# Fetching embedding rows from ScalarE's queue as well, in a gather-bound recommendation kernel on one Trainium2 core

## The chip, the cores and the metric

The kernel runs on one core of one Trainium2 chip. The metric is the device time of one execution in microseconds. The kernel before takes 32,128.78 us, the median of three runs between 32,128.46 and 32,131.62. A core has five engines, each with an instruction stream of its own: TensorE (PE, with its weight loads as PEld), VectorE (DVE), ScalarE (ACT), GpSimd (POOL) and SyncE (SP), which here only issues transfers. They meet through semaphores. A suffix q (SPq, ACTq) marks what an engine's sequencer does itself, such as issuing a transfer.

## The reference

The model is an attention network over a user's history of 200 items. With B = 16384 users, L = 200 history positions, D = 64 features per item, and 36 hidden units in the attention unit:

```python
def dice(x, alpha, axis):
    mean = jnp.mean(x, axis=axis, keepdims=True)
    var = jnp.var(x, axis=axis, keepdims=True)
    p = jax.nn.sigmoid((x - mean) * jax.lax.rsqrt(var + EPS))
    return x * (p + alpha * (1.0 - p))
u, it, c, h = u_emb[user], i_emb[item], c_emb[cate], i_emb[hist]   # h: 200 x 16384 x 64
itb = jnp.broadcast_to(it[None], h.shape)
feat = jnp.concatenate([h, itb, h - itb, h * itb], axis=-1)
a = dice(feat @ au_W1 + au_b1, au_alpha, axis=1)     # mean and variance over the 16384 users
w = a @ au_W2 + au_b2
cur = jnp.sum(w * jax.lax.stop_gradient(h), axis=0)  # sum over the 200 positions
z = jnp.concatenate([u, it, c, cur], axis=-1)
z = dice(z @ W1 + b1, alpha1, axis=0)
z = dice(z @ W2 + b2, alpha2, axis=0)
return z @ W3 + b3
```

The item table has 100,000 rows of 64 floats, 256 bytes each. Fetching 200 x 16384 = 3.28 million such rows from memory, in random order, is the bulk of the data movement (840 MB of the 882 MB that the profile counts).

## The kernel before

For each history position l the 16384 users are 128 tiles of 128 users. Sixteen tiles make one step, so that each l has ND = 8 steps; steps are numbered k = 8 l + c through the whole kernel, c from 0 to 7.

*Fetching.* A step's rows go into one of five buffers `rows`, [128 users, 16 tiles, 64 features]. GpSimd fetches a tile with one indirect gather of 128 rows (`gather`, line 117), its indices in `idx`, which SP loads once per l. In the steps named in `SIDES` (c = 3 and c = 7) the sixteenth tile comes another way, "by address": SP loads the item numbers of these two tiles as integers (`load_addresses`, line 135), DVE multiplies them by the row's 256 bytes (line 138), SP reads 16 of them at a time into its registers (line 258), and issues one transfer of 256 bytes per row (line 265) into a small tile `side`. ACT then copies `side` into the place in `rows` (line 301). So an l has 126 gathers by GpSimd and 256 single-row transfers by SP.

*Computing.* A step's rows are turned by DVE (`transpose`, line 146) into `hT`, [128, 1024], with features on the partitions. TensorE forms the hidden layer in the PSUM tile `px` from three products (line 151): `blk_h` with `hT`, `blk_i` with the turned item rows `itT`, and, a moment later, `blk_m` with `hm`. ACT copies `hT` to the PSUM tile `ph` (line 304); DVE multiplies that with `itT` to give `hm` (line 307). ACT adds the bias and writes `xs` (`hidden`, line 290), DVE takes statistics of `xs` (line 295). After the eighth step of an l, DVE and ACT make mean and variance into a scale and a shift (`moments`). Ten steps after its fetch (LAG) a step is weighed: ACT takes the sigmoid of `xs` with that scale and shift into the PSUM tile `pg` (line 278), then applies an affine with per-partition numbers, p (1 - alpha) w2 + alpha w2 (line 279); DVE multiplies by `xs` to give `y` (line 282); TensorE sums over the hidden units with the 0/1 matrix `blk_w` into `wb`; and DVE adds the bias, multiplies by `hT` and accumulates into `curT` (lines 286, 287).

*Order.* The order on each engine is the one in which `step` and `steps` write it down (`manual_schedule`); the framework adds semaphore waits where data or buffers require them, and each engine runs its own stream strictly in order. In step k that order is: fetch k; gate and weights of k - 10; hidden and statistics of k - 2; turn of k - 1; weighing of k - 10; product of k - 1; and after the last step of an l, its moments. SP's rows are asked for in front of each step (`ask`), 32 of a tile's 128 rows per step. For each DMA of SP the framework rotates over eight semaphores, so a row's transfer waits for the one eight before it.

*Loop.* 45 positions l form the body of a hardware loop that runs four times (line 406); the remaining 20 follow, and then the head: user and category gathers, two dense layers with their statistics, and the result.

Of the kernel before, what the change touches and what calls it, by code (L numbers as in the profile page):

```python
# [9 lines left out]
I32 = mybir.dt.int32  # L10
AF = mybir.ActivationFunctionType
ALU = mybir.AluOpType
PSUM = bass.MemoryType.PSUM

P = 128
D = 64
EPS = 1e-8
CH = 512
S = 32
CD = 2 * CH  # L20
LPB = 45
ROWS = 5
LAG = 10
XR = 9
IDX = 3
SIDES = (3, 7)
LOAD = 16
ROW = 4 * D
U8 = mybir.dt.uint8

# [2 lines left out]
def din_kernel(  # L33
# [24 lines left out]
    nc = tc.nc  # L58
    L, B = r_hist.shape
    NT = B // P  # L60
    TD = 2 * CD // P
    ND = NT // TD
    V = i_emb.shape[0]
# [2 lines left out]
    ZA = P // 2  # L66
    ZB = Z1 - ZA
    NS = len(SIDES)
    NC = NT - NS
    BODY = L - L % LPB if L > LPB else 0  # L70
    STATS = nc.vector.BN_STATS_DIM
# [5 lines left out]
    def make(name, *shape, dt=F32):  # L77
        return const.tile(list(shape), dt, name=name)
# [4 lines left out]
    def quarter(e, g, n=S):  # L83
        return slice((2 * e + g) * S, (2 * e + g) * S + n)
# [11 lines left out]
    ph = psum.tile([P, CD], F32, name="ph")  # L96
    pg = psum.tile([P, CD], F32, name="pg")
    wb = psum.tile([P, CD], F32, name="wb")

    rows = [make(f"rows{i}", P, TD, D) for i in range(ROWS)]  # L100
# [4 lines left out]
    hm = make("hm", P, CD)  # L105
# [2 lines left out]
    idx = [make(f"idx{i}", P, NC, dt=I32) for i in range(IDX)]  # L108
    ids = [make(f"ids{i}", P, NT, dt=I32) for i in range(3)]
    side = [make(f"side{i}", P, D) for i in range(3)]  # L110
    addr = [make(f"addr{i}", 1, NS * P, dt=I32) for i in range(3)]
    stats = [make(f"st{i}", P, 2 * ND, STATS) for i in range(3)]
    rstds = [make(f"rs{i}", P, 1) for i in range(3)]
    shifts = [make(f"sh{i}", P, 1) for i in range(3)]
# [28 lines left out]
    def transpose(dst, of):  # L143
        for i in range(2):
            for e in range(2):
                nc.vector.transpose(by_tile(dst[ts(e, D)], i), of[ts(i, D), :, ts(e, S)])  # L146

    def layer(dst, pairs, first=True, last=True):
        for i in range(2):
            for j, (lhsT, rhs) in enumerate(pairs):  # L150
                nc.tensor.matmul(  # L151
                    dst[:, ts(i, CH)], lhsT, rhs[:, ts(i, CH)],
                    start=(first and j == 0), stop=(last and j == len(pairs) - 1),
                    skip_group_check=not (first and last),
                )
# [9 lines left out]
    blk_h = make("blk_h", P, P)  # L165
    blk_i = make("blk_i", P, P)
    blk_m = make("blk_m", P, P)
    blk_w = make("blk_w", P, P)
    au_w = make("au_w", P, 4, A)
    au_bias = make("au_bias", P, 1)  # L170
    au_al = make("au_al", P, 1)
# [4 lines left out]

    def attention_weights():
        nc.vector.memset(eps, EPS)
        for t in (blk_h, blk_i, blk_m, blk_w, au_bias, au_al, au_w2):
            nc.vector.memset(t, 0.0)  # L180
        nc.sync.dma_start(au_bias2, au_b2.partition_broadcast(P))
        for e in range(2):
            w = au_W1.rearrange("(g d) a -> d g a", d=D)[e * S : (e + 1) * S]
            for g in range(2):
                r = quarter(e, g)
                nc.sync.dma_start(au_w[r], w)
                for q, (a0, n) in enumerate(halves):
                    c, a = quarter(q, g, n), slice(a0, a0 + n)
                    nc.vector.tensor_add(blk_h[r, c], au_w[r, 0, a], au_w[r, 2, a])
                    nc.vector.tensor_sub(blk_i[r, c], au_w[r, 1, a], au_w[r, 2, a])  # L190
                    nc.vector.tensor_copy(blk_m[r, c], au_w[r, 3, a])
                    nc.vector.memset(blk_w[r, quarter(q, g)], 1.0)
        for g in range(2):
            for q, (a0, n) in enumerate(halves):
                r, a = quarter(q, g, n), slice(a0, a0 + n)
                nc.sync.dma_start(au_bias[r], col(au_b1)[a])
                nc.sync.dma_start(au_al[r], col(au_alpha)[a])
                nc.sync.dma_start(au_w2[r], au_W2[a])
        nc.vector.tensor_scalar(au_1al, au_al, -1.0, 1.0, ALU.mult, ALU.add)
        nc.vector.tensor_mul(au_1al, au_1al, au_w2)  # L200
        nc.vector.tensor_mul(au_al, au_al, au_w2)


    w1a = make("w1a", P, 4, P)
# [10 lines left out]
    al1a, al1b, al12 = make("al1a", P, 1), make("al1b", P, 1), make("al12", P, 1)  # L215
    same_a = make("same_a", P, P)
    same_b = make("same_b", P, P)
    lanes = make("lanes", P, P, dt=I32)
    lane = make("lane", P, P, dt=I32)

    def head_weights():
        for t in (w1a, w1b, w2a, w2b, w3, bias2, al2):
# [28 lines left out]

    flat = i_emb.rearrange("v d -> (v d)").bitcast(U8)

    def rows_by_address(m, l, part, n):
        s, dst = m % NS, side[m % 3].bitcast(U8)
        for b in range(0, n, LOAD):
            p0 = part * n + b
            _, at = nc.values_load_multi_w_load_instructions(  # L258
                addr[l % 3][:, s * P + p0 : s * P + p0 + LOAD],
                engines=(mybir.EngineType.SP,), min_val=0, max_val=ROW * (V - 1),  # L260
                skip_runtime_bounds_check_because="the DMA checks the address against the table",
            )
            for j, a in enumerate(at):
                p = p0 + j
                nc.sync.dma_start(dst[p : p + 1], flat[ds(a, ROW)].rearrange("(o d) -> o d", o=1))  # L265

    def has_side(k):
        return k % ND in SIDES
# [7 lines left out]
    def gate(k):  # L276
        i = k // ND % 3
        nc.scalar.activation(pg, xs[k % XR], AF.Sigmoid, bias=shifts[i], scale=rstds[i])  # L278
        nc.scalar.activation(pg, pg, AF.Identity, bias=au_al, scale=au_1al)  # L279

    def weights(k):
        nc.vector.tensor_mul(y, pg, xs[k % XR])  # L282
        layer(wb, [(blk_w, y)])

    def weigh(k):
        nc.vector.scalar_tensor_tensor(wb, wb, au_bias2, hT[k % LAG], ALU.add, ALU.mult)  # L286
# [5 lines left out]
    def measure(k):  # L292
        l, c = divmod(k, ND)
        for i in range(2):
            nc.vector.bn_stats(stats[l % 3][:, 2 * c + i, :], xs[k % XR][:, ts(i, CH)])  # L295

    def turn(k):
        if has_side(k):
            l, c = divmod(k, ND)
            m = l * NS + SIDES.index(c)  # L300
            nc.scalar.copy(rows[k % ROWS][:, TD - 1], side[m % 3])
        transpose(hT[k % LAG], rows[k % ROWS])
        layer(px, [(blk_h, hT[k % LAG]), (blk_i, itT[k % ND])], last=False)
        nc.scalar.copy(ph, hT[k % LAG])  # L304

    def product(k):
        nc.vector.tensor_mul(hm, ph, itT[k % ND])  # L307
# [22 lines left out]
    def step(k, last=None):  # L330

        def has(j):
            return last is None or j <= last

        if has(k):
            fetch(k)
        if has(k - LAG):
            gate(k - LAG)
            weights(k - LAG)
        if has(k - 2):  # L340
            hidden(k - 2)
            measure(k - 2)
        if has(k - 1):
            turn(k - 1)
        if has(k - LAG):
            weigh(k - LAG)
        if has(k - 1):
            product(k - 1)
        if has(k - 2) and (k - 2) % ND == ND - 1:
            moments((k - 2) // ND)  # L350

    PER = ND // NS

    def ask(k, end):
        m, part = divmod(k + 1, PER)
        if m < end * NS:
            rows_by_address(m, m // NS, part, P // PER)

    def steps(l0, n, end):
        for k in range(n * ND):
            l, c = divmod(k, ND)
            if c == 0 and l + 1 < end:
                load_hist_ids((l + 1) % IDX, l0 + l + 1)
            if c == 2 and l + 1 < end:
                load_addresses((l + 1) % 3, l0 + l + 1)
            if c == 4 and l + 1 < end:
                scale_addresses((l + 1) % 3)
            ask(k, end)  # L370
            step(k)

    with tc.manual_schedule():
        load_ids(ids[0], r_item)
        load_hist_ids(0, 0)
        load_addresses(0, 0)
        load_ids(ids[1], r_cate)
        load_ids(ids[2], r_user)
        nc.gpsimd.iota(lanes, pattern=[[1, P]], base=P, channel_multiplier=-1)
        attention_weights()  # L380
        for t in (*hT, *xs, *side, hm):
            nc.vector.memset(t, 0.0)  # L382
        for t in curT:
            nc.vector.memset(t, 0.0)
        for i in range(3):
            nc.vector.memset(rstds[i], 0.0)
            nc.vector.memset(shifts[i], 0.0)  # L387
        nc.vector.bn_stats(stats[-1 % 3][:, 0, :], hm[:, :CH])
        for c in range(1, 2 * ND):
            nc.vector.tensor_copy(stats[-1 % 3][:, c, :], stats[-1 % 3][:, 0, :])  # L390
        scale_addresses(0)
        layer(px, [(blk_m, hm)])

        for c in range(ND + 1):
            if c < ND:
                for n in range(TD):
                    j = column(c, n)
                    gather(rows[c % ROWS], ids[0][:, j : j + 1], n, i_emb)
            if c:
                transpose(itT[c - 1], rows[(c - 1) % ROWS])  # L400
        nc.vector.memset(rows[-1 % ROWS], 0.0)
        ask(-1, L)
        head_weights()

    if BODY:
        with tc.For_i(0, BODY, LPB) as l0:  # L406
            with tc.manual_schedule():
                steps(l0, LPB, LPB + 1)

    K = (L - BODY) * ND  # L410
    za = [hT[(K - LAG + c) % LAG] for c in range(ND)]
# [140 lines left out]
```

## Time and profile before

| | us |
|---|---|
| median of three runs | 32,128.78 |
| the profiled execution's own time | 32,101.94 |
| its span, first to last instruction | 32,100.2 |
| busy: PE (with PEld beside it) | 15,661.4 (6,253.8) |
| busy: DVE | 14,921.9 |
| busy: ACT | 7,823.3 |
| busy: POOL | 24,139.4 |
| gathers of history rows: count, mean | 25,200, 0.944 |
| row transfers by SP: count, median to issue one | 51,200, 0.225 |

A row of the groups of instructions reads: line, engine, operation, output and input tiles, shape, count, then busy time and mean in ns, and the idle time of that engine just before these instructions with what ended most of it. "issue" is time in which the engine waited for nothing that the profile shows. A row of the view of one line gives the shortest, median and longest duration in ns. A row of windows gives the stretch in us, its length, the busy time and count of the engine, the granted TensorE clock, the DMA engines' busy share and GB/s. A row of the timeline gives the start in us, the length, the engine, and the idle time before it; several equal instructions in succession stand in one row, with their count. A row of waits gives who waited for whom, the sum in us, how often, and the longest.

### The profile page before, as it was taken

How to read it: one execution, taken by the hardware profiler on the slowest of the kernel's cores; microseconds unless marked ns; L12 is line 12 of the kernel's file. 1: busy time of each engine (PE TensorE's matmuls, PEld its weight loads, DVE VectorE, ACT ScalarE, POOL GpSimd, SP SyncE). 2: the span in 40 equal slices, each digit the busy share in tenths (PEclk: the TensorE clock that was granted, in tenths of full speed). 3: DMA queues.
4: the chain of work that ended last, by engine and by line, in shares of the span. 5: the costliest groups of instructions: out<-in, count | busy, mean ns of one | idle time of the engine just before them, and what ended most of it. 6: DMA issues, size and time to landing. Idle time of an engine off the chain costs nothing. (4 is left out here: it accounts for less than half of the span.)

```text
span 32100.2 us, 224464 instructions
## 1 busy us (share of the span) xinstructions
PE 15661.4 (49%) x26020; PEld 6253.8 (19%) x26020; DVE 14921.9 (46%) x18956; ACT 7823.3 (24%) x7481; POOL 24139.4 (75%) x25589
## 2 busy tenths in 40 slices
PE   4444444444444444444445444454444444445445
PEld 1111121111111111111112111121111211112111
DVE  4444444444444444444444444444444444444443
ACT  2222222222222222222222222222222222222222
POOL 7777777777777777777777777777777777777776
PEclk7777767776777777777777777777777777777777
DMA  1111111111111111111111111111111111111111
GB/s 28 28 28 28 28 28 28 28 27 28 28 28 28 28 28 28 28 27 28 28 28 28 28 28 28 28 28 28 28 28 28 28 28 28 28 28 28 28 28 22
DMA packets 958596, 881.57 MB, mean 27 GB/s; under 512 B 547488, under 2 KB 547688, under 8 KB 957032
## 3 DMA queue, kind: packets, MB, share of 16 engines
q0 software_dynamic: 818688, 839.97, 11.8%
q1 hardware_dynamic: 138056, 27.05, 0.4%
q14 instruction: 1352, 11.08, 0.1%
q8 instruction: 212, 3.47, 0.0%
q10 hardware_dynamic: 288, 0.00, 0.0%
HBM read 865.03 MB, written 0.13 MB: 27 GB/s over the span
## 5 line engine op out<-in xcount | busy, mean ns | idle before, releaser
L117 POOL DMA_INDIRECT rows<-in_L_rec_i_emb,idx x25200 | 23776.6, 944 | 7706.1 <-issue 7132.8
L151 PE MATMUL px<-hT,blk_h 128*128 128x512 f32 x6404 | 5661.5, 983 | 15033.9 <-DVE hT L146 15033.9
L146 DVE STREAM_TRANSPOSE hT<-rows 64x512 f32<-64x512 f32 x6404 | 4519.1, 706 | 12085.3 <-DMA rows<-in_L_rec_i_emb,idx 11421.6
L304 ACT COPY ph<-hT 128x1024 f32<-128x1024 f32 x1601 | 1627.1, 1016 | 18738.7 <-DVE hT L146 18738.7
L151 PEld LDWEIGHTS px<-hT,blk_h 128*128 128x128 f32 x6404 | 1816.6, 314 | 18047.2 <-issue 17233.6
L151 PE MATMUL px<-itT,blk_i 128*128 128x512 f32 x6404 | 4735.4, 832 | 0.0
L151 PE MATMUL wb<-y,blk_w 128*128 128x512 f32 x6440 | 3413.4, 657 | 1245.9 <-DVE y L282 1230.2
L295 DVE BATCH_NORM_STATS2 st<-xs 128x6 f32<-128x512 f32 x3204 | 2058.3, 684 | 3704.4 <-ACT xs L290 3704.4
L151 PE MATMUL px<-hm,blk_m 128*128 128x512 f32 x6408 | 3036.9, 596 | 38.1 <-DVE hm L382 36.4
L290 ACT ACTIVATE xs<-px,au_bias 128x1024 f32<-128x1024 f32 x1602 | 1781.6, 1112 | 4164.1 <-PE px L151 4164.1
L151 PEld LDWEIGHTS px<-itT,blk_i 128*128 128x128 f32 x6404 | 1862.1, 291 | 2859.9 <-issue 2859.9
L282 DVE TENSOR_TENSOR y<-pg,xs 128x1024 f32<-128x1024 f32 x1610 | 1954.9, 1214 | 736.6 <-ACT pg L279 736.4
L286 DVE SCALAR_TENSOR_TENSOR wb<-wb,au_bias,hT 128x1024 f32<-128x1024 f32 x1610 | 2081.1, 1293 | 82.2 <-PE wb L151 30.0
L287 DVE TENSOR_TENSOR curT<-wb,curT 128x1024 f32<-128x1024 f32 x1610 | 1971.2, 1224 | 54.8
L278 ACT ACTIVATE pg<-xs,sh,rs 128x1024 f32<-128x1024 f32 x1610 | 1937.3, 1203 | 79.9 <-DVE sh L387 42.7
L307 DVE TENSOR_TENSOR hm<-ph,itT 128x1024 f32<-128x1024 f32 x1601 | 1942.5, 1213 | 0.0
L279 ACT ACTIVATE pg<-pg,au_al,au_1al 128x1024 f32<-128x1024 f32 x1610 | 1895.1, 1177 | 54.1
L151 PEld LDWEIGHTS wb<-y,blk_w 128*128 128x128 f32 x6440 | 1307.8, 207 | 2976.1 <-issue 1538.0
L151 PEld LDWEIGHTS px<-hm,blk_m 128*128 128x128 f32 x6408 | 1195.9, 191 | 1686.8 <-issue 1236.5
L278 ACT ACT_TABLE_LOAD x206 | 264.3, 1283 | 77.5 <-PEq L406 57.4
L160 ACT ACT_TABLE_LOAD x203 | 260.4, 1283 | 7.5 <-PE pg L461 4.0
L160 ACT ACTIVATE std<-var,eps 128x1 f32<-128x1 f32 x201 | 59.2, 294 | 710.6 <-DVE var L327 710.6
(147 smaller groups left out, 1531.7 us busy)
## 6 DMA issues: line engine op xcount, KB each, us to landing
side<-in_L_rec_i_emb SPq DMA_DIRECT2D x51200, 0.2 KB
rows<-in_L_rec_i_emb,idx POOLq DMA_INDIRECT x25200, 2.4
idx<-in_r_hist SPq DMA_DIRECT2D x200, 63.0 KB
addr<-in_r_hist SPq DMA_DIRECT2D x200, 1.0 KB
rows<-in_L_rec_i_emb,ids POOLq DMA_INDIRECT x128, 2.4
rows<-in_L_rec_c_emb,ids POOLq DMA_INDIRECT x128, 2.3
rows<-in_L_rec_u_emb,ids POOLq DMA_INDIRECT x128, 2.4
w1a<-in_L_rec_W SPq DMA_DIRECT2D x4, 32.0 KB
```

The costliest lines, as they stand in the source:

```text
L117: nc.gpsimd.indirect_dma_start(out=dst[:, n, :], out_offset=None, in_=table, in_offset=bass.IndirectOffsetOnAxis(ap=ids, axis=0),)
L146: nc.vector.transpose(by_tile(dst[ts(e, D)], i), of[ts(i, D), :, ts(e, S)])
L151: nc.tensor.matmul(dst[:, ts(i, CH)], lhsT, rhs[:, ts(i, CH)], start=(first and j == 0), stop=(last and j == len(pairs) - 1), skip_group_c ...
L278: nc.scalar.activation(pg, xs[k % XR], AF.Sigmoid, bias=shifts[i], scale=rstds[i])
L279: nc.scalar.activation(pg, pg, AF.Identity, bias=au_al, scale=au_1al)
L282: nc.vector.tensor_mul(y, pg, xs[k % XR])
L286: nc.vector.scalar_tensor_tensor(wb, wb, au_bias2, hT[k % LAG], ALU.add, ALU.mult)
L287: nc.vector.tensor_add(curT[k % ND], wb, curT[k % ND])
L290: nc.scalar.activation(xs[k % XR], px, AF.Identity, bias=au_bias)
L295: nc.vector.bn_stats(stats[l % 3][:, 2 * c + i, :], xs[k % XR][:, ts(i, CH)])
L304: nc.scalar.copy(ph, hT[k % LAG])
L307: nc.vector.tensor_mul(hm, ph, itT[k % ND])
```

## The change

Two more tiles of each l are fetched by address, and ACT issues these. `SIDES` becomes (1, 3, 5, 7): SP takes the sixteenth tile of steps 1 and 5, ACT that of steps 3 and 7. GpSimd's gathers fall from 126 to 124 per l. In each step ACT issues four groups of eight rows (`GROUP`), two after the sigmoid and two after `hidden`; each group begins with a load of eight addresses into ACT's registers. The transfers increment a semaphore of the destination tile (`landed`), three tiles (`aside`) taking turns, and carry no waits of their own; before the copy of a tile ACT waits until all 128 rows have counted in, and clears the semaphore. The body of the loop ends with that wait for the tile still under way. SP's requests start two steps earlier (`AHEAD`), because its tiles are now used in steps 1 and 5. The addresses of all four tiles lie in one tile `addrs`, loaded and scaled in one instruction each as before.

ACT loses two instructions per step. The affine after the sigmoid is folded into TensorE's sum: `wb` becomes `blk_p` times p x plus `blk_x` times x, with the two per-partition numbers multiplied into the 0/1 matrix beforehand. The copy of `hT` to `ph` becomes a product of `hT` with a unit matrix, placed in front of the products into `px`. Both are fp32 products of [128 x 128] with two halves of 512 columns. The integer tiles `lanes` and `lane` of the head move into buffers that are free at that time.

```diff
-SIDES = (3, 7)
+BY_SP = (1, 5)
+BY_ACT = (3, 7)
+SIDES = (1, 3, 5, 7)
 LOAD = 16
+GROUP = 8
...
+    aside = [make(f"aside{i}", P, D) for i in range(3)]
+    landed = [tc.alloc_semaphore(f"landed{i}") for i in range(3)]
+    addrs = make("addrs", 2 * S + 1, NS * P, dt=I32)
+    addr = [addrs[i * S : i * S + 1] for i in range(3)]
...
+        nc.vector.tensor_scalar_mul(blk_x, blk_p, au_al)
+        nc.vector.tensor_scalar_mul(blk_p, blk_p, au_1al)
+        nc.vector.tensor_copy(unit, lanes)
+        nc.vector.tensor_single_scalar(unit, unit, float(P), ALU.is_equal)
...
+    def addresses(l, s, p0, n, engine):
+        _, at = nc.values_load_multi_w_load_instructions(
+            addr[l % 3][:, s * P + p0 : s * P + p0 + n],
+            engines=(engine,), min_val=0, max_val=ROW * (V - 1),
...
+        return [flat[ds(a, ROW)].rearrange("(o d) -> o d", o=1) for a in at]
+
+    def rows_by_sync(m, part, n):
+        l, j = divmod(m, NB)
+        s, dst = SIDES.index(BY_SP[j]), side[m % 3].bitcast(U8)
+        for p0 in range(part * n, part * n + n, LOAD):
+            for j, row in enumerate(addresses(l, s, p0, LOAD, mybir.EngineType.SP)):
+                nc.sync.dma_start(dst[p0 + j : p0 + j + 1], row)
+
+    keys = {}
+
+    def rows_by_scalar(m, part):
+        l, j = divmod(m, NA)
+        s, dst = SIDES.index(BY_ACT[j]), aside[m % 3].bitcast(U8)
+        key = keys.setdefault(m, f"rows{next(serial)}")
+        for j, row in enumerate(addresses(l, s, part * GROUP, GROUP, mybir.EngineType.Activation)):
+            p = part * GROUP + j
+            dma = nc.scalar.dma_start(dst[p : p + 1], row).then_inc(landed[m % 3], 16)
+            tc.no_tile_sem_insts.add(dma.ins.name)
+            tc.add_to_no_dep_group(key, dma.ins)
+
+    def await_rows_by_scalar(m):
+        if m in keys:
+            fence = nc.scalar.wait_ge(landed[m % 3], 16 * P)
+            tc.declare_fence(fence.ins, group=keys.pop(m))
+            nc.scalar.sem_clear(landed[m % 3])
...
     def gate(k):
         i = k // ND % 3
         nc.scalar.activation(pg, xs[k % XR], AF.Sigmoid, bias=shifts[i], scale=rstds[i])
-        nc.scalar.activation(pg, pg, AF.Identity, bias=au_al, scale=au_1al)
 
     def weights(k):
         nc.vector.tensor_mul(y, pg, xs[k % XR])
-        layer(wb, [(blk_w, y)])
+        layer(wb, [(blk_x, xs[k % XR]), (blk_p, y)])
...
-            m = l * NS + SIDES.index(c)
-            nc.scalar.copy(rows[k % ROWS][:, TD - 1], side[m % 3])
+            if c in BY_ACT:
+                m = l * NA + BY_ACT.index(c)
+                await_rows_by_scalar(m)
+                of = aside[m % 3]
+            else:
+                of = side[(l * NB + BY_SP.index(c)) % 3]
+            nc.scalar.copy(rows[k % ROWS][:, TD - 1], of)
         transpose(hT[k % LAG], rows[k % ROWS])
+        layer(ph, [(unit, hT[k % LAG])])
         layer(px, [(blk_h, hT[k % LAG]), (blk_i, itT[k % ND])], last=False)
-        nc.scalar.copy(ph, hT[k % LAG])
...
             gate(k - LAG)
             weights(k - LAG)
+        if has(k):
+            scalar_rows(k, 0)
         if has(k - 2):
             hidden(k - 2)
             measure(k - 2)
+        if has(k):
+            scalar_rows(k, 1)
         if has(k - 1):
             turn(k - 1)
...
-    PER = ND // NS
+    AHEAD = ND // NB - 1 - BY_SP[0]
 
     def ask(k, end):
-        m, part = divmod(k + 1, PER)
-        if m < end * NS:
-            rows_by_address(m, m // NS, part, P // PER)
+        m, part = divmod(k + 1 + AHEAD, ND // NB)
+        if m < end * NB:
+            rows_by_sync(m, part, P * NB // ND)
+
+    def scalar_rows(k, slot):
+        m, part = divmod(k, ND // NA)
+        n = P * NA // ND // GROUP
+        for i in range(n)[slot::2]:
+            rows_by_scalar(m, part * n + i)
...
-        ask(-1, L)
+        for k in range(-1 - AHEAD, 0):
+            ask(k, L)
...
                 steps(l0, LPB, LPB + 1)
+                await_rows_by_scalar(LPB * NA - 1)
```

## The prediction

> **What bounds the kernel now.** I read the page's rows first, then GpSimd's timeline, then the instructions of the two lines that fetch rows by address, then the waits. The page:
>
> ```profile
> span 32100.2 us, 224464 instructions
> ...
> POOL 7777777777777777777777777777777777777776
> ...
> L117 POOL DMA_INDIRECT rows<-in_L_rec_i_emb,idx x25200 | 23776.6, 944 | 7706.1 <-issue 7132.8
> ```
>
> POOL shows 75% busy, evenly, and its idle time is put down to "issue", its own dispatching. So the busy share understates it: every gather has 0.944 us of work and 0.30 us of issue. Two windows of 50 us and the end of one loop turn show the pace:
>
> ```profile
> 10037.00:10087.00 50.00, 37.80 (x41) 0.69 0.13 28
> 10100.00:10150.00 50.00, 37.81 (x41) 0.69 0.12 26
> ```
>
> ```profile
> 7238.83 0.94 POOL L117 DMA_INDIRECT rows<-in_L_rec_i_emb,idx  x1 [0.30 <-issue]
> 7240.08 0.94 POOL L117 DMA_INDIRECT rows<-in_L_rec_i_emb,idx  x1 [0.30 <-issue]
> 7249.02 0.94 POOL L117 DMA_INDIRECT rows<-in_L_rec_i_emb,idx  x1 [8.00 <-issue]
> ```
>
> Start to start a gather takes 1.249 us, as 7238.83 to 7240.08. The gathers number 25,584 (25,200 for history, 384 for the other tables): 25,584 x 1.249 = 31,954 us of a span of 32,100. Only four gaps between them exceed 1.4 us (8.9, 7.2, 7.2, 4.0 us): the three turns of the loop and its exit. The rest is the 2.9 us ahead of the first gather and some 135 us of head after the last. Gathers set the end; nothing that the others do inside a step shows. The waits agree: consumers wait for rows, on DVE and then on ACT.
>
> ```profile
> DVE hT L146 <- DMA rows<-in_L_rec_i_emb,idx: 11421.6, 1498, 9.3
> ACT ph L304 <- DVE hT L146: 18738.7, 1601, 13.5
> ACT xs L290 <- PE px L151: 4164.1, 1397, 3.8
> ```
>
> Each l has 8 steps and 126 gathers, so a step is now 126 / 8 x 1.249 = 19.67 us.
>
> **Fewer gathers.** Two gathers fewer for each of 200 l: 400 x 1.249 = 499.6 us saved, if the pace stays and nobody else becomes the bound. The new step is 124 / 8 x 1.249 = 19.36 us. Does more row traffic slow a gather? In the first of the two windows SP issued 121 row transfers, in the second none: both hold 41 gathers, and the spacings are 1.2491 and 1.2486 us. A second stream at the same price would cost 24,800 x 0.0005 = 12 us; I take 0 to 12, value 3.
>
> **ACT's new work.** Per step it issues 32 rows in four groups of 8, each led by a load of 8 addresses into registers (helper `addresses`). SP does the same now, in groups of 16:
>
> ```profile
> L265 SPq MOVE side<-in_L_rec_i_emb x51200: 29/29/38, 48.4 to 31504.5; - x200
> L265 SPq DMA_DIRECT2D side<-in_L_rec_i_emb x51200: 224/225/362, 48.5 to 31504.5; - x200
> ...
> L258 SPq TENSOR_LOAD <-addr x3200: 1130/1229/1483, 47.1 to 31498.1; - x189
> ...
> 10006.81 25.05 SPq L265 DMA_DIRECT2D side<-in_L_rec_i_emb  x64
> ```
>
> From one row's issue to the next is 0.32 us (move 0.029, DMA 0.225, dispatch), and a load of 16 addresses stretches that once by 1.30: 16 x 0.32 + 1.30 = 6.42, 0.40 a row, as 25.05 / 64 says. No row shows a load of 8. Above, it costs the 1.30 of 16. Below, the Trainium skill's DMA: Bandwidth & Descriptors, "Latency and other measured facts", gives a floor of about 0.6 us for such a load. ACT's step is 32 x 0.32 = 10.2 us plus 4 x 0.6 to 1.3: 12.6 to 15.4 us. I take 15.4, as the load's row is measured and its split per address is not.
>
> ACT's own arithmetic beside it: the sigmoid 1.20, `hidden` 1.11, side copies 4 x 0.23 / 8 = 0.12, two table loads per l 2 x 1.28 / 8 = 0.32, the square root 0.04: 2.8 us. The affine (1.18) and the copy to `ph` (1.02) go:
>
> ```profile
> L304 ACT COPY ph<-hT 128x1024 f32<-128x1024 f32 x1601 | 1627.1, 1016 | 18738.7 <-DVE hT L146 18738.7
> ...
> L279 ACT ACTIVATE pg<-pg,au_al,au_1al 128x1024 f32<-128x1024 f32 x1610 | 1895.1, 1177 | 54.1
> ```
>
> Is arithmetic added to issuing, or under it? Line 301's semaphore instructions start at 10072.7, when `hidden` has just started at 10072.69 and runs to 10073.80: ACT's sequencer goes on under a running ACTIVATE. So the sum is 15.4 us plus what an ACTIVATE waits before it starts; not overlapped at all it is 18.2. Both are under 19.36. What queues behind the rows: `hidden` of step k-2 stands after 16 of them (7.7 us), the side copy and the next sigmoid after the other 16; `measure` and the next turns on DVE wait for these. A turn can be late by about three steps, some 58 us, before POOL waits, because `rows` has five buffers. Only throughput counts. The `landed` wait stands about one step after its last row was issued, against some 2.4 us to landing for a gather: zero cost. At a turn of the loop ACT now ends at 7226.9, 13 us before POOL's last gather at 7240.1, with the copy to `ph`; that goes, and the groups in its place end about as late: zero. If ACT's slack were gone, each us over 19.36 costs 1600 us.
>
> **The shared descriptor generator.** A rule that speaks against this: the skill's Perfetto Trace Analysis, "DMA Instruction — HWDGE (DVE, Sync)", says that such a DMA locks one generator, shared by the two issuing engines, for exclusive use. SP issues 256 rows per l too. If all 0.225 us are lock, then while both issue a row takes 0.45, not 0.32. SP needs 256 x 0.45 + 16 x 1.30 = 136 us of 154.9, so ACT is contended 88% of the time: 32 x (0.88 x 0.45 + 0.12 x 0.32) + 5.2 = 19.1 us before any wait, at the bound or over it. The trace has one place where both issue together:
>
> ```profile
> L519 ACTq DMA_DIRECT2D out<-res x2: 373/396/418, 32078.5 to 32092.8; - x2
> ...
> L513 SPq DMA_DIRECT2D out<-res x8: 315/426/432, 32078.5 to 32094.1; - x8
> ```
>
> At 32078.46 and again at 32092.80 both begin within 0.01 us; SP takes 0.354 and 0.315, ACT 0.418 and 0.373. The second in line ends 0.06 us later, not a whole DMA later. By the row ACT pays at most 0.06 a row: 32 x 0.06 = 1.9 us, 17.3 in all, and the end is not moved. I take the row; these are two pairs, of another shape, so the rule keeps a chance.
>
> **TensorE's new work.** Per step four more instructions for `ph` and four for `wb`; an fp32 product is two. One step's 16 now run from 10004.96 to 10013.74. In the slow start one follows the other by 0.85 us (10065.95, 10066.80, 10067.66 in another step), later four take 1.88: 4 x 0.85 + 4 x 0.47 = 5.3 us more, 14.1 of 19.36. In the chain `ph` is ready about 5.6 us after the turn begins, where ACT's copy ended 3.9 after; DVE reaches the product at 5.4. So `xs` is some 3.5 us later, and its statistics, which end 11.1 us after the turn begins (10003.39 to 10014.50), end at about 14.6: inside the step, with 4.7 us of cover. Granted clock is 0.72 now; were every instruction at the slow 0.85, 24 take 20.4 us (a rival below).
>
> **SP, start and end.** SP's count stays, 256 rows per l, asked two steps earlier (`AHEAD`) because their tiles are turned two steps earlier; the scaled addresses come at step 4 as before. 128 rows take 51 us of the six steps left: zero. Before the loop 64 more rows, 26 us, beside 160 us of gathers; some weight loads and memsets move ahead of the loop, 0 to 10 us once. Sum: 32,101.9 (the profiled execution's own time; span 32,100.2) - 499.6 + 3 = 31,605. The median of the runs is 26.8 above that execution: 32,128.8 - 499.6 + 3 = 31,632.
>
> **The rivals.** *Partial gain.* ACT a little over the step, or POOL caught at loop turns and at the square root, where ACT waits for DVE: 0.2 us per step is 320 us back, 31,950. For it: ACT's margin is 1 to 4 us. Against: transition between hidden and bound is narrow. *ACT becomes the bound, slower.* The generator is exclusive and the 2.8 us of arithmetic are not covered: 19.1 + 2.8 = 21.9 us a step, (21.9 - 19.36) x 1600 = 4,060 more, 35,700; half of that contention gives 20.1 and 32,800. It decides from 19.67 us a step on, the old step. It also covers a dearer address load on ACT, from 2.4 us each. *TensorE binds.* 20.4 us a step: 31,632 + 1.04 x 1600 = 33,300; needs the fast half of each burst, visible now, to vanish. *The change doesn't do what it says:* the pace isn't per gather. Against it: 41 in each window, unchanged by SP.
>
> **How the numbers follow.** Hidden everywhere: 0.78, 31,632, own range 31,600 to 31,700. Partial: 0.07, of which 0.05 faster. ACT binds: 0.12; TensorE: 0.02; no effect: 0.01. A measurement here tells 0.2% (64 us) from nothing. Faster 0.83, within 0.2% 0.03, slower 0.14. The range 31,595 to 31,950 holds the first case and most of the second, some 0.83, with the unknown load price and contention as far as they stay hidden.
>
> **What would show it.** Right: 24,800 history gathers still 1.249 us apart, POOL's gaps still four, ACT's row issue near 0.32 us, and ACT idle 2 to 6 us per step before `hidden`. Wrong: POOL waiting for DVE or ACT at the first gather of a step, ACT's DMA instructions near 0.45 us or its loads over 2 us, SP's lengthened beside them, or TensorE without idle time.

## The result, and the profile after

The changed kernel takes 31,645.5 us, the median of four runs (31,617.0 to 31,647.4); beside them the kernel before took 32,129.9 (four runs, 32,128.5 to 32,131.6). The ratio is 0.9847, with a 95% interval of 0.983 to 0.9864: 484.4 us less, where the prediction said 496.8 less and 31,632, in a range of 31,595 to 31,950.

The page of the changed kernel (the execution of 31,617.0 us):

```profile
span 31615.1 us, 357535 instructions
...
PE 20448.2 (65%) x38864; PEld 8357.2 (26%) x38864; DVE 15015.4 (47%) x18963; ACT 4479.6 (14%) x4670; POOL 23766.1 (75%) x25189
...
L125 POOL DMA_INDIRECT rows<-in_L_rec_i_emb,idx x24800 | 23403.2, 944 | 7593.5 <-issue 7032.1
L159 PE MATMUL ph<-hT,unit 128*128 128x512 f32 x6404 | 5658.4, 1029 | 10498.9 <-DVE hT L154 10498.9
...
L323 ACT ACTIVATE xs<-px,au_bias 128x1024 f32<-128x1024 f32 x1602 | 1784.3, 1114 | 14626.1 <-PE px L159 12323.9
```

There are 400 gathers fewer, each still 0.944 us, and POOL's idle time is still put down to its own issue. GpSimd in the same two windows as before (start and end, length, POOL's busy time and count, granted clock, DMA share, GB/s):

```profile
10037.00:10087.00 50.00, 37.76 (x41) 0.83 0.13 28
10100.00:10150.00 50.00, 37.81 (x41) 0.80 0.12 27
```

41 gathers in 50 us, as before. Over the whole trace they start 1.2488 us apart on average (before: 1.2484), gaps over 1.5 us left out. The first turn of the loop in GpSimd's timeline:

```profile
7128.21 0.94 POOL L125 DMA_INDIRECT rows<-in_L_rec_i_emb,idx  x1 [0.30 <-issue]
7129.46 0.94 POOL L125 DMA_INDIRECT rows<-in_L_rec_i_emb,idx  x1 [0.30 <-issue]
7139.70 0.94 POOL L125 DMA_INDIRECT rows<-in_L_rec_i_emb,idx  x1 [9.30 <-issue]
```

The gaps at the three turns and the exit are 10.2, 8.5, 8.5 and 3.9 us where they were 8.9, 7.2, 7.2 and 4.0: 3.8 us more in all. No other gap between gathers is over 1.5 us. So the saving of 499.5 us (400 x 1.2488) arrives, less 3.8 at the turns, some 10 us in the pace of the gathers (25,184 x 0.0004) and 1 us more after the last gather: 485.1 between the two profiled spans.

What ACT issues, by line (shortest, median and longest duration in ns), with SP's load and rows beside it:

```profile
L291 ACTq MOVE aside<-in_L_rec_i_emb x51200: 29/29/38, 52.1 to 31139.5; - x200
L291 ACTq DMA_DIRECT2D aside<-in_L_rec_i_emb x51200: 217/218/596, 52.2 to 31139.6; - x200
```

```profile
L268 ACTq TENSOR_LOAD <-addrs x6400: 709/817/1073, 51.3 to 31136.3; - x194
L268 SPq TENSOR_LOAD <-addrs x3200: 1132/1230/1459, 51.3 to 31016.3; - x189
```

```profile
L280 SPq DMA_DIRECT2D side<-in_L_rec_i_emb x51200: 224/228/447, 52.7 to 31022.6; - x200
```

A row costs ACT 0.31 us from one to the next (SP 0.32), a load of eight addresses 0.82. The waits of the changed kernel (who waited for whom: sum in us, times, longest):

```profile
ACT xs L323 <- PE px L159: 12323.9, 1195, 17.3
DVE st L328 <- ACT xs L323: 7172.9, 1600, 5.9
POOL rows L125 <- issue: 7142.1, 23320, 9.3
```

POOL appears with its own issue and with no consumer of `rows`. The first of these lines must be read with care: issuing does not count as busy, so ACT's idle time before `hidden`, 10.3 us on average, holds the two groups of rows that it issues there, some 7.2 us. What is left is time to spare. In the stretch from 12,000 to 18,400 us it is 3.3 us on average from the last row ahead of `hidden` to the load behind it.

### The profile page after: what moved, and what is told of

It is laid out like the page before. It is cut to its first block, busy times and chain, and to the rows that moved or that the text cites. A ratio compares the mean times of both kernels' runs of the same rounds, so it can differ in the third digit from the quotient of the medians.

```text
span 31615.1 us, 357535 instructions
## 1 busy us (share of the span) xinstructions
PE 20448.2 (65%) x38864; PEld 8357.2 (26%) x38864; DVE 15015.4 (47%) x18963; ACT 4479.6 (14%) x4670; POOL 23766.1 (75%) x25189
## 5 line engine op out<-in xcount | busy, mean ns | idle before, releaser
L125 POOL DMA_INDIRECT rows<-in_L_rec_i_emb,idx x24800 | 23403.2, 944 | 7593.5 <-issue 7032.1
L159 PE MATMUL ph<-hT,unit 128*128 128x512 f32 x6404 | 5658.4, 1029 | 10498.9 <-DVE hT L154 10498.9
L159 PEld LDWEIGHTS ph<-hT,unit 128*128 128x128 f32 x6404 | 1688.5, 295 | 13506.4 <-DVE hT L154 13334.4
L159 PE MATMUL px<-hT,blk_h 128*128 128x512 f32 x6404 | 3936.6, 702 | 0.0
L159 PE MATMUL wb<-y,blk_p 128*128 128x512 f32 x6440 | 3329.8, 599 | 455.3 <-DVE y L315 455.3
L159 PE MATMUL px<-itT,blk_i 128*128 128x512 f32 x6404 | 3368.8, 608 | 0.0
L159 PE MATMUL wb<-xs,blk_x 128*128 128x512 f32 x6440 | 3307.3, 595 | 51.5 <-PEq L455 39.9
L159 PEld LDWEIGHTS px<-itT,blk_i 128*128 128x128 f32 x6404 | 1374.9, 215 | 1925.3 <-issue 1925.3
L159 PEld LDWEIGHTS wb<-y,blk_p 128*128 128x128 f32 x6440 | 1212.0, 191 | 2081.7 <-issue 1445.9
L159 PEld LDWEIGHTS wb<-xs,blk_x 128*128 128x128 f32 x6440 | 1228.3, 191 | 1603.9 <-issue 1597.9
```

Source lines behind the costliest of these rows:

```text
L125: nc.gpsimd.indirect_dma_start(out=dst[:, n, :], out_offset=None, in_=table, in_offset=bass.IndirectOffsetOnAxis(ap=ids, axis=0),)
L159: nc.tensor.matmul(dst[:, ts(i, CH)], lhsT, rhs[:, ts(i, CH)], start=(first and j == 0), stop=(last and j == len(pairs) - 1), skip_group_c ...
```

## Experiments

Twelve runs were made. Besides "does it hold", three questions stand behind them: which of the change's two parts does the work, how far ACT is from being the bound, and what the second stream of rows costs the first.

**1. TensorE's part alone.** The kernel before, with the affine and the copy to `ph` given to TensorE, and no rows moved.

```diff
-        nc.scalar.activation(pg, pg, AF.Identity, bias=au_al, scale=au_1al)
...
-        layer(wb, [(blk_w, y)])
+        layer(wb, [(blk_x, xs[k % XR]), (blk_p, y)])
...
+        layer(ph, [(unit, hT[k % LAG])])
...
-        nc.scalar.copy(ph, hT[k % LAG])
```

> The kernel before with only TensorE's part of the change: the affine and the copy to ph as products, still 126 gathers per l and no rows by ACT. Theory (the gathers' pace sets the end): 25,584 x 1.249 us plus the same start and tail, so 32,130 +- 10, though ACT's busy time falls by about 3,500 us and PE's rises by about 5,000. Rival (the shorter ACT work is part of the gain): some of the 484 us appears here, 31,900 or less.

Measured: 32,126.8 us (ten runs, 32,124.6 to 32,127.7) beside 32,124.9 on the same chip; ratio 1.0001, 0.9991 to 1.001. The busy row of its page:

```profile
PE 20839.7 (65%) x38864; PEld 8536.7 (27%) x38864; DVE 14932.9 (46%) x18960; ACT 4279.1 (13%) x4270; POOL 24164.2 (75%) x25589
```

ACT's busy time falls from 7,823 to 4,279 us and PE's rises from 15,661 to 20,840, and the time is the same: neither engine set the end.

**2. The rows alone.** The changed kernel with the affine and the copy back on ACT.

```diff
+        nc.scalar.activation(pg, pg, AF.Identity, bias=au_al, scale=au_1al)
...
-        layer(wb, [(blk_x, xs[k % XR]), (blk_p, y)])
+        layer(wb, [(blk_p, y)])
...
-        layer(ph, [(unit, hT[k % LAG])])
...
+        nc.scalar.copy(ph, hT[k % LAG])
```

> The changed kernel with ACT's affine and its copy to ph put back on ACT: 124 gathers, 256 rows per l by ACT, TensorE as before. Theory (ACT's sequencer issues rows under a running ACTIVATE; only a step over 19.36 us counts): issue 14.2 us, plus the waits before the copy and between sigmoid and affine, some 18 us, still hidden: 31,645 +- 15. Rival (arithmetic and issue add up on ACT, and TensorE's part is what makes room): 14.2 + 2.8 + 2.2 = 19.2 us, and the wait for the turn on top, 20 us or more: 32,700 or more.

Measured: 31,645.0 us (31,643.3 to 31,659.2), ratio 0.9852, 0.9835 to 0.9868: as the changed kernel. The whole gain comes from the gathers that are not made. By these two runs TensorE's part could be left out. Experiments 7 and 8 show how thin that reading is.

**3. Dearer groups on ACT.** Groups of two addresses instead of eight, so 16 loads a step.

```diff
-GROUP = 8
+GROUP = 2
```

> The changed kernel with rows issued in groups of 2, so 16 address loads per step in place of 4. From the traces a load of 16 took 1.23 us and one of 8 took 0.82, so one of 2 is estimated at 0.50; with 0.23 more for the first row after a load, 0.1 of dispatch and 0.31 per row a group takes 1.44 us and a step 23.1. Theory (issue alone counts, arithmetic hidden): (23.1 - 19.36) x 1600 = 6,000 over the changed kernel, about 37,600, POOL waiting. Rival (arithmetic adds): 25.9 us, about 42,100. If ACT is far from being the bound for another reason: 31,645.

Measured: 44,952.6 us, in one run. The rival that ends on the slow side does exist, and this is what it looks like. Its waits, and its load of two addresses on ACT:

```profile
ACT xs L323 <- issue: 19120.4, 1546, 13.1
...
POOL rows L125 <- DVE hT L154: 13056.0, 768, 18.8
```

```profile
L268 ACTq TENSOR_LOAD <-addrs x25600: 653/767/1039, 51.3 to 44555.6; - x199
```

POOL now waits for DVE's turns, 13,056 us in all, and `hidden` is late because of ACT's own issue, no longer because of TensorE. The mechanism was the theory's; the size was not. I had put a load of two at 0.50 us, from the loads of 16 and of 8; it took 0.77. That is the whole difference: the longer first row after a load (0.45 us) was in the estimate. A group of two is then 1.70 us where 1.44 was expected, and 16 of them are 27.2 us of a step of 27.7.

**4. Groups of four.** The same edit with `GROUP = 4`.

> The changed kernel with rows issued in groups of 4, eight address loads per step. From the run with groups of 2 a group of 2 takes 1.70 us, and each further row 0.31: 2.31 us, 18.5 a step, and the 0.5 us that the run with groups of 2 had over its 16 groups makes 19.0. Theory (issue alone counts, and nothing below 19.36 us shows): 31,645, at most 31,750, with ACT almost without idle time. Rival (the sigmoid, hidden and the rest add their 2.8 us): 21.3 to 21.8 us a step, 34,700 or more.

On the chip of the first run the kernel before itself took 46,611.6 us, and this one 51,730.7 (ratio 1.1096, 1.1042 to 1.1151). There, in stretches, the moves, transfers and address loads of ACT and SP took some 0.7 us each. The row issue of that run:

```profile
L291 ACTq MOVE aside<-in_L_rec_i_emb x51200: 2/29/1472, 105.1 to 51057.1; - x200
L291 ACTq DMA_DIRECT2D aside<-in_L_rec_i_emb x51200: 2/222/1468, 105.2 to 51059.2; - x200
```

A register move has a median of 29 ns and a longest of 1,472, where the changed kernel's longest is 38 elsewhere. The kernels with more instructions on ACT lost more. Instructions that arrive late at the engine would look like this, but that is not shown; what ailed that chip was not looked into. On another chip:

> Groups of 4 once more, for the same reason. On a chip where the kernel before takes 32,130: a load of 4 took 0.59 us in the first run's undisturbed stretches, so a group of 4 takes about 2.13 us and a step 17.0 plus 0.5. Theory (issue alone counts): 31,645, at most 31,700. Rival (arithmetic adds its 2.8 us): 20.3 us, 33,200. On a chip like the first: over 50,000 us.

Measured: 31,632.4 us (31,619.0 and 31,645.8), ratio 0.9853, 0.9834 to 0.9873. Hidden, as the theory said; a load of four has a median of 0.587 us.

**5. ACT's rows left out.** GpSimd's 124 gathers and SP's two tiles stay; ACT's two tiles of each l hold zeros, so 51,200 of the history's rows are missing from the output.

```diff
-        for j, row in enumerate(addresses(l, s, part * GROUP, GROUP, mybir.EngineType.Activation)):
-            dma = nc.scalar.dma_start(dst[p : p + 1], row).then_inc(landed[m % 3], 16)
...
-            fence = nc.scalar.wait_ge(landed[m % 3], 16 * P)
...
-            nc.scalar.sem_clear(landed[m % 3])
```

> The changed kernel without the fetch of ACT's rows: neither the address loads nor the transfers nor the wait for them; the two tiles hold zeros, so that part of the computation is left out. Theory (the rows cost nothing but a slightly slower gather, 1.2488 against 1.2484 us): 31,632 to 31,636, a gain of about 10 us over the changed kernel's 31,645. Rival (ACT's rows cost time in the steps or at the loop's turns): a gain of 50 us or more.

Measured: 31,637.4 us (31,635.5 to 31,639.4). No gain of 50 us shows. How much ACT's 51,200 transfers cost the others is not settled by these times: against the changed kernel's runs near 31,645 it is 8 us, but its runs near 31,617 are 20 us shorter than this one, as the pace of the gathers moves between executions. In the traces the gathers start 1.2496 us apart here and 1.2499 in experiment 2, whose profiled run took 31,646: 5 to 6 us for 25,184 gathers. The longer gaps at the turns of the loop are there without ACT's rows too, and in experiment 2 without TensorE's part, and not in experiment 1. So they belong to what these kernels share; it was not tried which part.

**6. A fifth tile.** Half of it by SP, half by ACT, so that GpSimd makes 123 gathers for each l.

```diff
-BY_ACT = (3, 7)
-SIDES = (1, 3, 5, 7)
+BY_ACT = (3, 6, 7)
+BOTH = 6
+SIDES = (1, 3, 5, 6, 7)
...
+    half = [make(f"half{i}", P // 2, D) for i in range(3)]
...
+                if c == BOTH:
+                    nc.scalar.copy(rows[k % ROWS][: P // 2, TD - 1], half[l % 3])
+                    nc.scalar.copy(rows[k % ROWS][P // 2 :, TD - 1], of[P // 2 :])
+                    of = None
```

> A fifth tile of each l by address, its first 64 rows by SP and its last 64 by ACT: 123 gathers per l, five groups of 8 per step on ACT, SP's groups of 16 two or three a step. Theory: each gather less per l is worth 200 x 1.249 = 250 us as long as ACT's step (5 x 3.55 + 0.5 = 18.2 us) and SP's l (320 x 0.40 = 128 us) stay under 19.2 and 153.6 us: 31,645 - 250 = 31,395 +- 20. Rival (SP and ACT together are near a common limit of row transfers, a generator or a DMA ring): 640 rows per l in place of 512 lengthen the row issues and the time stays at 31,600 or rises.

That run fell on the slow chip as well: 53,351.1 us beside 46,611.6. Again, with the changed kernel beside it, on a chip where the kernel before takes 32,103.1:

> The kernel with a fifth tile once more, as the chip of its first run gave 46,612 us for the kernel before too and stretches in which ACT and SP took 0.7 us for every single instruction. On a chip where the kernel before takes 32,130: theory 31,645 - 250 = 31,395 +- 20; rival (a common limit of row transfers) 31,600 or more. On a chip like the first: again over 50,000 us.

> The changed kernel itself, unedited, beside the other two on the same chip. Where the kernel before takes 32,130: 31,645 +- 5. On a chip like that of the two runs before, where instructions reach ACT and SP slowly in stretches: ACT's 32 moves and 32 transfers per step are instructions that the kernel before doesn't have on ACT, so it is slower than the 46,612 of the kernel before, 48,000 to 52,000.

Measured: the changed kernel 31,618.8 us (31,617.9 to 31,619.4). With five tiles the four runs were 31,442, 31,464, 31,742 and 31,742, a median of 31,602.8 and a ratio of 0.9859, 0.9814 to 0.9903. In the profiled run of 31,442 us, `hidden` starts 24 us after the last gather of its rows at first and 67 us after it at the end of the first pass through the loop's body, and the turn to the second pass then costs 50.5 us. In the stretch from 2,000 to 6,800 us ACT issues for 18.1 us a step and spends 1.1 us between groups: 19.2 us, exactly GpSimd's step. I had put the issuing at 17.75. So ACT was at its limit, or something that both row streams share was. What sets the runs of 31,742 apart is not known; none of them left a trace. Groups of 16 on ACT tell the two causes apart (the loop that deals the groups out to the steps changes with it, to two or three a step):

```diff
-GROUP = 8
+GROUP = 16
```

> Five tiles by address again (123 gathers for each l), with ScalarE's 2.5 tiles issued in groups of 16 addresses instead of 8. Theory (in the five-tile run with groups of 8, ScalarE itself had become the limit: its step had grown to some 19.2 us): a group of 16 takes some 1.23 us for the load + 0.33 for the first row's extra and the wait + 16 x 0.307 = 6.5 us; 20 groups for each l are 130 us, 16.2 us a step instead of some 17.8, against GpSimd's 19.2 to 19.4. ScalarE keeps a reserve, and the time is the changed kernel's less 200 x 1.25 = 250 us: 31,395 where the kernel before takes 32,128, 31,369 where it takes 32,103, within 20 us and steady over the runs. Rival (not ScalarE but a common limit on how fast rows can be fetched by address beside the gathers): groups of 16 change nothing, 31,440 to 31,740 and scattered as with groups of 8.

Measured: 31,365.5 us (31,363.7 to 31,366.8) beside 32,101.4; ratio 0.9771, 0.9754 to 0.9787. The theory's figure was 31,369. It was ACT, and five tiles in groups of 16 beat both kernels: 736 us of the 749 that 600 gathers take. Its load of 16 on ACT:

```profile
L270 ACTq TENSOR_LOAD <-addrs x4000: 1184/1211/1532, 53.0 to 30880.7; - x191
```

From 2,000 to 6,800 us ACT now issues for 16.6 us a step and has 2.6 between groups, where it had 18.1 and 1.1. `hidden` no longer drifts: it starts 13 to 21 us after the last gather of its rows through the first pass.

**7. The arithmetic back on ACT, where ACT is the limit.** Experiment 3 with the edit of experiment 2.

> Groups of two addresses, so that ScalarE's issuing sets the step (44,953 us with TensorE's part), and the affine and the copy to ph back on ScalarE: does arithmetic there cost time when ScalarE is the limit? Theory (two instructions of arithmetic in succession stop the sequencer: the second waits until the first is done; where the rows were moved alone, the rows after the sigmoid started 2.08 us after its start, with TensorE's part 0.74 to 0.92): the affine adds some 1.2 us a step and the copy some 1.0, together 2.2 x 1600 = 3,500: 48,500 us, within 500. Rival (arithmetic runs under the issuing, as the unchanged time of the rows alone could be read): nothing is added, 44,950 to 45,400.

Measured: 51,510.1 us, in one run, 6,557 more than with TensorE's part, 4.10 us a step. That is more than the theory said (2.2) and far from the rival (nothing). The timeline of ACT shows what was left out; the number in brackets is the idle time before an instruction, with what ended it:

```profile
15051.19 12.80 ACTq L285 DMA_DIRECT2D aside<-in_L_rec_i_emb  x16
15064.34 0.24 ACT L334 COPY rows<-side 128x64 f32<-128x64 f32 x1 [12.91 <-issue]
15067.54 1.02 ACT L337 COPY ph<-hT 128x1024 f32<-128x1024 f32 x1 [2.95 <-DVE hT L154]
15068.49 1.20 ACT L306 ACTIVATE pg<-xs,sh,rs 128x1024 f32<-128x1024 f32 x1
15069.73 1.18 ACT L307 ACTIVATE pg<-pg,au_al,au_1al 128x1024 f32<-128x1024 f32 x1
15070.53 12.62 ACTq L285 DMA_DIRECT2D aside<-in_L_rec_i_emb  x16
```

ACT copies the sixteenth tile into `rows` and must then copy `hT` to `ph`, but `hT` is what DVE makes of `rows`. So ACT stands for 2.95 us until DVE has turned the step that ACT has only just completed, and no row is issued meanwhile. Between the last row of one group and the load of the next, ACT loses 5.70 us in a step with a side copy (0.35 with TensorE's part), 2.23 in a step without (0.07), and 7.3 where the moments come in between (2.05). An l has four, three and one of these steps: (4 x 5.35 + 3 x 2.16 + 5.3) / 8 = 4.15 us a step, against the 4.10 measured. Two pieces make most of it: the copy, the sigmoid and the affine in succession, some 2.2 us in every step, as the theory said, and the wait for DVE in every other step, 1.5 us a step on average.

**8. The same at five tiles in groups of 16.**

> Five tiles by address with groups of 16, with the affine and the copy to ph back on ScalarE (the kernel without TensorE's part). Theory (the arithmetic is added to the issuing): ScalarE's step is 2.5 groups x 6.5 + 0.2 + 2.2 + some 0.4 for the copies and the moments = 19.05 us against GpSimd's 19.2, so that it is at the edge: 31,400 to 31,700 us where the kernel with TensorE's part takes 31,366, the gathers held up here and there. Rival (the arithmetic is under the issuing, ScalarE's step stays 16.4): 31,366, within 15.

Measured: 35,186.9 us (35,181.5 to 35,188.5), ratio 1.0951, 1.0936 to 1.0967, where with TensorE's part it is 31,365.5. Both expectations were too low; the sum of the theory lacked the same wait. The waits of this kernel:

```profile
POOL rows L127 <- DVE hT L156: 3911.4, 1416, 7.5
...
ACT ph L352 <- DVE hT L156: 2909.9, 1001, 9.8
```

ACT waits for DVE in five steps of eight, 2.9 us each time, and POOL waits for DVE in its turn.

With that the rows alone (experiment 2) read differently. In the stretch from 12,000 to 18,400 us ACT there issues for 14.4 us a step and spends 5.0 between groups, which fills the step of 19.4. Its blocks of 5.70 and 2.23 us are as long as in experiment 7, where ACT is the limit; only the block at the moments has time to spare, 1.9 us on average, 0.24 us a step. `hidden` does not drift there: that kernel stands just inside the limit. The timeline of that kernel has the same wait:

```profile
15025.54 0.24 ACT L334 COPY rows<-side 128x64 f32<-128x64 f32 x1 [6.66 <-DMA side<-in_L_rec_i_emb]
15025.82 2.88 DVE L154 STREAM_TRANSPOSE hT<-rows 64x512 f32<-64x512 f32 x4 [5.62 <-ACT rows L334]
...
15028.73 1.02 ACT L337 COPY ph<-hT 128x1024 f32<-128x1024 f32 x1 [2.95 <-DVE hT L154]
```

The changed kernel issues for 14.4 us a step as well, and what it must spend between groups is the 0.6 us of experiment 3: some 4.4 us to spare. At four tiles TensorE's part buys no time, only room; with a fifth tile that room is worth 3,821 us.

## Why the prediction was right

*What bounds the kernel.* Right. The time follows the number of gathers: 126, 124 and 123 for each l give 32,102, 31,619 and 31,366 us in runs with nearly the same pace, 483 and 253 us apart for 500 and 250 us of gathers.

*Fewer gathers.* The term of 499.6 us was 499.5. The gain fell 12 us short, 484.4 against 496.8, and between the two profiled spans as well. There the gathers' slower pace cost some 10 us, where the sum took 3 from a range of 0 to 12, and the turns of the loop cost 3.8, for which it had zero. How much of the 10 us is the price of the second stream is open, as the pace moves by more than that between executions of one kernel; experiment 5 suggests 5 to 8.

*ACT's issuing.* Predicted 15.4 us a step, as 32 x 0.32 + 4 x 1.30; measured 14.4. A row was 0.31 instead of 0.32, the load of eight 0.82 instead of up to 1.30. Against these stands the first row after a load, 0.45 instead of 0.22, which no view of the kernel before could show for ACT. The lower end that came from the Trainium skill, DMA: Bandwidth & Descriptors, "Latency and other measured facts" (about 0.6 us), would have given 12.6 us; the measured load lies between the two ends. It does not fall steadily with the number of addresses: 1.21 us for 16, 0.82 for 8, 0.59 for 4, 0.77 for 2. The sign named for this, ACT idle for 2 to 6 us before `hidden`, came as 3.3.

*Arithmetic under the issuing.* The prediction left open whether ACT's 2.8 us come on top, 15.4 to 18.2, both hidden. Right for what was left on ACT: a single ACTIVATE stops the sequencer for 0.06 to 0.12 us. For several in succession it would have been wrong, since each waits for the one before it and the sequencer stands with them (2.23 us for the copy, the sigmoid and the affine in experiment 7). The step "the affine (1.18) and the copy to `ph` (1.02) go" was under-priced: what goes with them is 4.1 us of ACT's sequencer, some 1.5 of it the wait for DVE. It did not touch the forecast, as ACT's margin held either way. But the profile before had it: ACT's copy to `ph` waited 18,738.7 us for DVE there, at no cost, because ACT had nothing else to do. With rows to issue the same wait is a stop.

*The shared descriptor generator.* The prediction trusted the two pairs in the trace over the rule, and that held. By the Trainium skill's Perfetto Trace Analysis, "DMA Instruction — HWDGE (DVE, Sync)", a row on ACT was to take 0.45 us while SP issues, if all of SP's 0.225 us are lock. ACT's DMA instruction has a median of 218 ns where none of SP's runs and 222 where one does at its start (means 250 and 255); SP's is 228 either way, and 228 in experiment 5, where ACT issues no rows. A loss of 4 to 6 ns a row is under the 60 ns that were allowed for.

*TensorE.* Its burst was to take 14.1 us of the step; in the changed kernel's timeline it runs from the first of these lines to the end of the second, 12.6 us:

```profile
10008.12 3.78 PE L159 MATMUL ph<-hT,unit 128*128 128x512 f32 x4 [7.95 <-DVE hT L154]
...
10019.67 1.02 PE L159 MATMUL wb<-y,blk_p 128*128 128x512 f32 x2
```

The slow start is in it (four in 3.78 us, against 1.88 later), and the fast half did not vanish; the granted clock rose from 0.72 to 0.81, as it did with TensorE's part alone (0.81) and not with the rows alone (0.73). `ph` is ready in time: DVE reaches the product at 10,012.03, 5.4 us after the turn begins, as foreseen.

*The rivals.* "ACT becomes the bound" is a real mechanism with the point of decision where it was put, at GpSimd's step; experiments 3, 7 and 8 are on its far side. Contention was not what leads there. "Partial gain" was nearer than its 0.07 said: without TensorE's part the changed kernel would have stood at its edge. With it, the margin was 4.4 us, where the sum allowed 1 to 4.

*The profiled execution and the median.* The 27 us between them came back: 31,617 against 31,645. By the traces it is the pace of the gathers: 1.2488 us in both traces of the changed kernel, near 31,617, and 1.2499 in those of experiment 2 and of groups of four, which ran near 31,646 with as many gathers. No execution of the changed kernel itself near 31,645 left a trace. What sets the pace was not found; a contention of a few us cannot be read from one profile against another while it moves.

## What to carry to other kernels

When an engine is given a stream of transfers to issue, count what its sequencer loses, not what its arithmetic unit is busy: a wait that cost nothing while the engine was idle anyway becomes a stop in the stream, and a round trip to another engine that answers the work just done costs its full length each time (2.95 us here). Taking such a step off the engine can show no gain at all at the present size and decide the next one, so test it where the engine is near its limit before calling it useless. And a load of addresses into registers pays for itself by its size: going from 8 to 16 a load took ACT's issuing from 18.1 to 16.6 us a step at five tiles, and turned four runs 300 us apart into four within about 3 us.

## What was not expected of the hardware

- The first row that ACT issues after a load of addresses takes 0.45 us, the others 0.22; a load of two addresses (0.77 us) takes longer than one of four (0.59).
- The pace of the same gathers differs by 0.001 us between executions, 27 us over the kernel.
- On one chip the moves, transfers and address loads of ACT and SP took some 0.7 us each in stretches, and the kernel before took 46,612 us instead of some 32,125. In the trace of groups of four there, a gather itself still took 0.944 us.
